# A convolution loop on one core: state products set between two channels, input loaded with batch innermost, gelu written in runs of four

## The chip, the core and the metric

The kernel runs on one core of a Trainium2 chip. The metric is the time on the device in microseconds (us), from launch to the last output, as the median of the runs shown. All inputs lie in HBM; the host only reorders and copies them before the launch, which isn't timed.

## The reference

The input `r` is [8, 2048, 512] (batch, time, channel), float32. Two residual blocks follow each other:

```
x = r
x = x + LN(gelu(causal_conv(LN(x), K) + D * LN(x)))     # block 1
x = x + LN(tanh(LN(x) Wo^T + c_final Uo^T + bo))          # block 2
```

In block 1 every channel has its own kernel K of 2048 taps, given by a state space of 64 complex states; the reference computes it with FFTs. In block 2 `c_final` is the end state of a gated recurrence that runs over the first axis (here the 8 batch entries) with sigmoid and tanh gates, for all 2048 positions at once:

```
c = f * c + i * g,   f, i = sigmoid(x W^T + c U^T + b),   g = tanh(x W^T + c U^T + b)
```

LN subtracts the mean and divides by the standard deviation over the 512 channels, with no learned scale.

## The kernel before, in words

**Set-up and statistics** (`stats`, line 409 on). The powers of the state matrix, the first taps of K and other constants are made by short chains of small instructions. Beside them `stats(j)` takes the time axis in 16 chunks of 128 positions (positions on partitions): two loads bring a chunk's 8 rows per position from `xr` into `xs` (line 421), VectorE's `bn_stats` (L424) and ScalarE's accumulating copies (L429, L433) give mean and 1 / std of each row, which stay in `mu1` and `rs1`. For the first two groups of channels `u`, the normalized input, is made here from `xc` (L442 on GpSimd, L443 on VectorE), split in a float16 high part (L446, ScalarE) and the float16 rest (L447, GpSimd). A scheduler orders the instructions of this stage on each engine.

**The convolution loop** takes 32 channels at a time: 16 groups `g`. A chunk's output is a Toeplitz product of the chunk with the first 128 taps (tile `t`, a load from `kpad`, L494) plus a product of the state before the chunk (tile `x`) with the powers that read the state out (tile `m`). All matrix products are done with both sides split in hi and lo, so three matmuls each (`mm3`, lines 388 to 390: hi hi, lo hi, hi lo). Within a group the work goes by 16 slots, and inside the loop the order on TensorE, ScalarE, VectorE and GpSimd is the order in which the program is written. A slot `s_` of group `g` has:

- `chain_step(g + 1, s_)`: the state after chunk s_ of the next group. Three products of the transition matrix `at` with the state before are added in PSUM (`pxt`); `split` then writes x's high half (L83, ScalarE) and its low half (L84, VectorE). Its third product reads the low half of the previous state.
- `conv_out` in even slots: gelu of the four channels finished in the two slots before (L531, ScalarE), from PSUM `pyt` [position, channel, chunk and batch] into `y` [position, chunk and batch, channel]. The pattern walks PSUM in storage order, so it writes one float32 every 64 bytes. After 16 channels `y` is stored to `y_d`.
- `conv_mm(g, s_)`: two channels, 12 products.
- `tap_step` in slots 1 to 12: the next group's tile `m`, doubled from 4 to 128 columns by three products of 64 to 512 columns, evicted by L83 and L84.
- `chain_in(g + 1, s_ + 1)`: three products of the input matrix `bm` with `u`, the first part of the next `pxt`.
- `norm_x(g + 2, ...)`: the input of the group after next, loaded in `xg` (L453), in four parts: mean off (L466, GpSimd), times 1 / std (L468, VectorE), high part `u` (L470, ScalarE), low part (L472, GpSimd; VectorE for group 2). Two parts fall in a slot, so that in a steady group the even slots have GpSimd's first part and ScalarE's `u`, the odd ones VectorE's and GpSimd's second.

`xr` has, for a chunk, position and group, the 8 batch entries outside and the 32 channels inside; `u` has channels outside and batch inside. So L470 and L472 read `xg` with a step of 128 bytes.

Group 0 has no chain and no taps beside it, group 14 has no `norm_x` but splits weights of the recurrence, group 15 (`conv_last`) goes in two parts of the sequence. All loads and stores of the loop go through SyncE's queue, in an order that the scheduler plans and where a transfer waits for its buffer, and everything behind it in the queue waits too.

**The recurrence** then runs over 8 blocks of 256 positions and 8 steps each (`prep`, `norm`, `turn`, `scan`, `head`). It reads `y_d` and isn't touched by the change.

Of the kernel before, what the change touches and what calls it, by code (L numbers as in the profile page):

```python
# [45 lines left out]
def s4_gated_block(ctx, tc, a, dbg=None):  # L46
# [28 lines left out]
    # long-lived results of the set-up  # L75
# [21 lines left out]
    with ExitStack() as sctx:  # L97
# [10 lines left out]
        # large temporaries sit where later tiles of the convolution will  # L108
# [277 lines left out]
    def mm3(out, w, x, start=True, stop=True):  # L386
        """out (+)= w^T x with both sides as hi + lo: hi hi + hi lo + lo hi"""
        T.matmul(out, lhsT=w(0), rhs=x(0), start=start, stop=False)  # L388
        T.matmul(out, lhsT=w(1), rhs=x(0), start=False, stop=False)  # L389
        T.matmul(out, lhsT=w(0), rhs=x(1), start=False, stop=stop)  # L390

# [12 lines left out]
    with ExitStack() as cctx:  # L404
# [4 lines left out]
        def stats(j):  # L409
            """mean and 1 / std of the rows of chunk j (VectorE and ScalarE share the batch),  # L410
            and u of the first two groups"""
# [6 lines left out]
            for i in range(2):  # L418
                tag = ("y", "xg", "y", "xg", "u2")[(2 * j + i) % 5]
                xh.append((cr if tag == "xg" else ce if tag == "u2" else cb).tile([P, NG, HB, G], F32, name="xs", tag=tag, bufs=1 if tag == "u2" else 2))  # L420
                dma(out=xh[i], in_=a["xr"][j, :, :, i * HB : (i + 1) * HB])
            row = lambda b: xh[b // HB][:, :, b % HB, :]
# [4 lines left out]
            for b in range(na):  # L427
                jk = xp.tile([P, NG, G], F16, name="jk", bufs=1)
                S.activation(jk, row(nd + b), AF.Copy, accum_out=sm[:, 0, b : b + 1])  # L429
            S.mul(sm[:, 1, 0:na], sm[:, 0, 0:na], -1.0 / H)  # L430
            for b in range(na):
                jk = xp.tile([P, NG, G], F16, name="jk", bufs=1)
# [16 lines left out]
        def load_x(g):  # L449
            us[g] = (cb, cr, ce)[g % 3].tile([P, NJ, 2, G, NB], F16, name="u", tag=f"u{g % 3}", bufs=1)  # L450
            for jq in range(NJ // JQ):
                xg = cr.tile([P, JQ, NB, G], F32, name="xg")
                dma(out=xg, in_=a["xr"][jq * JQ : (jq + 1) * JQ, :, g].rearrange("j p b h -> p j b h"))  # L453
                xgs[g, jq] = xg

        def norm_x(g, jp, part):
            """u = LN(x) as [time, chunk, channel, batch], split in hi and lo, in four parts"""
# [5 lines left out]
            x3, xv = xg.rearrange("p j b h -> p (j b) h"), xg.rearrange("p j b h -> p j h b")  # L463
            bc = lambda m: m[:, js, :].rearrange("p j b -> p (j b)")[:, :, None].to_broadcast([P, JP * NB, G])
            if part == 0:
                Q.tensor_tensor(x3, x3, bc(mu1), ALU.subtract)  # L466
            elif part == 1:
                V.tensor_tensor(x3, x3, bc(rs1), ALU.mult)  # L468
            elif part == 2:
                S.activation(u[:, js, 0], xv, AF.Copy)  # L470
            else:
                (V if g == 2 else Q).tensor_tensor(u[:, js, 1], xv, u[:, js, 0], ALU.subtract)  # L472

        def chain_in(g, j):
            """B u of chunk j, the first part of the state after it"""
# [6 lines left out]
        def chain_step(g, j):  # L482
            x, pxt = xs_[g], pxs.pop((g, j))
            if j:
                mm3(pxt, lambda i: at16[:, i, :], lambda i: x[:, j - 1, i, :], start=False)
            split(x[:, j, 0, :], x[:, j, 1, :], pxt)

        def load_taps(g):
            """first-chunk Toeplitz blocks, and the start of the powers that read the state out"""
# [23 lines left out]
        def conv_mm(g, c):  # L513
            """two channels of group g"""
            u, x = us[g], xs_[g]
            if c % 2 == 0:
                pys[g] = py.tile([P, 4, NJ * NB], F32, name="pyt")
            for hg in (2 * c, 2 * c + 1):
                sl, hm = 2 * g + hg // HS, hg % HS
                t0, m = t0s[sl], ms[sl]  # L520
                o = pys[g][:, hg % 4, :]
                mm3(o, lambda i: t0[:, i, :, hm], lambda i: u[:, :, i, hg, :], stop=False)
                mm3(o[:, NB:], lambda i: m[:, i, :, hm], lambda i: x[:, :, i, hg * NB : (hg + 1) * NB], start=False)

        def conv_out(g, c4):
            """gelu of four channels"""
# [4 lines left out]
            S.activation(y[:, :, h4 : h4 + 4].rearrange("p c h -> p h c"), pys[g], AF.Gelu, scale=unsc)  # L531
# [4 lines left out]
        def conv_last(g):  # L536
            """the last group in two parts of the sequence: the first positions can go on earlier"""
            u, x = us[g], xs_[g]
            yt = {}
            for j0, j1, hn in ((0, JF, HS), (JF, NJ, 4)):  # L540
                n = j1 - j0
                for sl in (2 * g, 2 * g + 1):
# [4 lines left out]
                    for h0 in range(0, HS, hn):  # L547
# [7 lines left out]
                        S.activation(y[:, :, h0 : h0 + hn].rearrange("p c h -> p h c"), pyt, AF.Gelu, scale=unsc)  # L555
# [25 lines left out]
        # when the weights' halves are split and loaded: {group: {slot: (splits, loads)}}  # L581
# [10 lines left out]
        for g in range(NG):  # L592
# [16 lines left out]
            with tc.manual_schedule(engines=MAN):  # L609
# [13 lines left out]
                for s_ in range(NJ):  # L623
# [12 lines left out]
                    if nn:  # L636
                        # the loads of group 3 come late: its parts are taken in fewer slots
                        d = ND1 if g == 1 else 0
                        while norms and s_ >= d and (s_ == NJ - 1 or len(norms) > 4 + 2 * NJ * (NJ - 1 - s_) // (NJ - d)):
                            norm_x(g + 2, *norms.pop(0))  # L640
# [15 lines left out]
    def lnstat(src, tag):  # L656
        """mean and 1 / std of the rows of each [P, ...] view in src"""
# [16 lines left out]
    def prep(q, t, cjs=(0, 1)):  # L674
        """x1"""
# [16 lines left out]
    def norm(q, t, cjs=(0, 1)):  # L692
        """its normed rows"""
# [5 lines left out]
    def turn(q, t, cjs=(0, 1)):  # L699
        """the normed rows with channels on partitions, split in hi and lo"""  # L700
# [11 lines left out]
    def scan(q, t, mr=range(KT)):  # L712
        """a step of the recurrence for a block of positions"""
# [33 lines left out]
    def zbank(q):  # L747
        """a PSUM bank of products with positions on partitions (after the scan its banks are free)"""
# [111 lines left out]
def _arrays(d):  # L860
    """The inputs, laid out as the kernel reads them (copies and reorderings only)."""
# [16 lines left out]
    a["xr"] = r[:, :, ::-1].transpose(1, 2, 3, 0, 4)  # L878
# [20 lines left out]
```

## Time and profile before

| | |
|---|---|
| runs before | 2988.52 us median of 3 (2986.27 to 2988.61) |
| span of the profiled execution, first to last instruction | 2986.2 us, 59439 instructions |
| its stages, from the first starts of their lines | set-up and statistics to about 158 us, loop to 643 us, recurrence to the end |
| busy over the span | PE 95%, DVE 56%, ACT 38%, POOL 24% |
| mean granted TensorE clock | 0.982 of full |
| DMA | 311.32 MB, mean 104 GB/s |

The profile shows one execution. The times of the three runs are listed without naming the one that was profiled; its span lies 2.3 us under their median. PE is TensorE's matmuls and PEld its weight loads, DVE is VectorE, ACT ScalarE, POOL GpSimd, SP SyncE. A group of instructions is listed by line, engine, output and input tile with shapes, then count, busy time, mean of one, and the idle time of the engine just before them with what ended it. Matmuls overlap, so their spacing is read from their starts and not from their durations. A row of a table by stretches has the stretch and its length, then busy us and count for PE, PEld, DVE, ACT and POOL, and the granted clock, the share of time in which the DMA engines were busy, and what they moved in GB/s.

### The profile page before, as it was taken

The page shows a single profiled execution, that of the slowest core. Times are in us where ns is not written, and L with a number is a line of the kernel's source. Part 1 is how long each engine was busy: PE and PEld are TensorE (multiplying, and loading weights), DVE is VectorE, ACT ScalarE, POOL GpSimd, SP SyncE. Part 2 cuts the span into 40 slices and gives each one's busy share as a digit, 9 for nine tenths or more (in the row PEclk, how much of TensorE's full clock was granted, in tenths as well). Part 3 has the DMA queues.
Part 4 walks back from the last instruction along what each step waited for, and adds up shares of the span by engine and source line. Part 5 has one row for each costly group of instructions (what it writes and reads, how often), then busy time and mean ns, then how long its engine had stood idle before and what let it go on. Part 6 is the DMA issues. An engine that isn't in the chain of part 4 may idle for free.

```text
span 2986.2 us, 59439 instructions
## 1 busy us (share of the span) xinstructions
PE 2844.7 (95%) x25044; PEld 2346.3 (79%) x25044; DVE 1670.0 (56%) x3674; ACT 1130.7 (38%) x2288; POOL 730.1 (24%) x723
## 2 busy tenths in 40 slices
PE   3589999899999999999999999999999999999998
PEld 2367777788888888788888888887888788888884
DVE  7766666656645555655555555555555655563336
ACT  8888888842222222222222222222222222222221
POOL 5757777600100111111111111111111111110013
PEclk9699999989999999999999999999999999999999
DMA  8977676765522222322232222222222322221003
GB/s 223 280 216 213 204 214 202 203 174 127 107 50 58 71 72 71 78 71 72 71 93 71 72 72 72 71 72 71 72 71 72 85 72 71 71 79 43 29 29 103
DMA packets 520916, 311.32 MB, mean 104 GB/s; under 512 B 282310, under 2 KB 442568, under 8 KB 520648
## 3 DMA queue, kind: packets, MB, share of 16 engines
q1 hardware_dynamic: 520216, 306.99, 38.8%
q8 instruction: 196, 3.21, 0.5%
q14 instruction: 72, 0.59, 0.1%
q10 hardware_dynamic: 432, 0.52, 0.1%
HBM read 206.28 MB, written 101.19 MB: 103 GB/s over the span
## 4 chain that ended last, share of the span: by engine, by line
PE 71%; issue 10%; ACT 6%; DVE 5%; DMA 3%; POOL 2%; POOLq 0%; SPq 0%; ACTq 0%; DVEq 0%
PE pfi L390 12%; PE pfi L388 12%; PE pfi L389 12%; PE pgg L388 6%; PE pgg L389 6%; PE pgg L390 6%; PE pz L389 3%; PE pz L390 3%; PE pz L388 3%; ACT u L470 2%; ACT y L531 2%; PE pt L708 2%; PE pxt L390 1%; DVE xg L468 1%; PE pyt L389 1%
## 5 line engine op out<-in xcount | busy, mean ns | idle before, releaser
L389 PEld LDWEIGHTS <-w 128*128 128x128 f16 x5808 | 568.0, 98 | 73.4 <-issue 6.4
L388 PEld LDWEIGHTS <-w 128*128 128x128 f16 x5808 | 568.0, 98 | 72.3 <-issue 0.7
L390 PEld LDWEIGHTS <-w 128*128 128x128 f16 x5808 | 568.0, 98 | 72.1
L388 PE MATMUL pfi<-xt,w 128*128 128x256 f16 x2048 | 559.8, 273 | 0.7 <-ACT xt L83 0.7
L389 PE MATMUL pfi<-xt,w 128*128 128x256 f16 x2048 | 559.9, 273 | 0.0
L390 PE MATMUL pfi<-xt,w 128*128 128x256 f16 x2048 | 559.6, 273 | 0.1
L388 PE MATMUL pfi<-ch,w 128*128 128x256 f16 x1792 | 489.1, 273 | 5.1 <-ACT ch L742 5.1
L390 PE MATMUL pfi<-ch,w 128*128 128x256 f16 x1792 | 489.0, 273 | 0.1
L389 PE MATMUL pfi<-ch,w 128*128 128x256 f16 x1792 | 489.1, 273 | 0.0
L731 ACT ACTIVATE gate<-pfi,bias 128x256 f32<-128x256 f32 x512 | 214.8, 471 | 644.0 <-PE pfi L390 643.3
L737 DVE SCALAR_TENSOR_TENSOR a<-gate,cd 128x256 f32<-128x256 f32 x224 | 118.1, 527 | 508.5 <-ACT gate L731 508.5
L667 POOL TENSOR_TENSOR rsh<-rsh,nhalf 128x2 f32<-128x2 f32 (+1 forms) x65 | 45.1, 693 | 1458.6 <-DVE rsh L666 1436.4
L742 ACT ACTIVATE ch<-cd 128x256 f16<-128x256 f32 x256 | 106.6, 416 | 530.6 <-DVE cd L741 530.6
L388 PE MATMUL pgg<-xt,w 128*128 128x256 f16 x1024 | 279.1, 273 | 0.0
L389 PE MATMUL pgg<-xt,w 128*128 128x256 f16 x1024 | 279.1, 273 | 0.0
L390 PE MATMUL pgg<-xt,w 128*128 128x256 f16 x1024 | 279.1, 273 | 0.0
L389 PE MATMUL pgg<-ch,w 128*128 128x256 f16 x896 | 244.3, 273 | 0.0
L388 PE MATMUL pgg<-ch,w 128*128 128x256 f16 x896 | 244.3, 273 | 0.0
L390 PE MATMUL pgg<-ch,w 128*128 128x256 f16 x896 | 244.2, 273 | 0.0
L83 ACT ACTIVATE xt<-pt 128x512 f16<-128x512 f32 x128 | 75.8, 597 | 316.6 <-PE pz L390 218.6
L779 POOL TENSOR_TENSOR x1r<-x1r,h 128x512 f32<-128x512 f32 x124 | 181.2, 1480 | 41.1 <-DVE h L778 41.1
L740 DVE SCALAR_TENSOR_TENSOR gate<-gate,gate 128x256 f32<-128x256 f32 x256 | 108.9, 426 | 137.4 <-ACT gate L731 137.4
(303 smaller groups left out, 5964.2 us busy)
## 6 DMA issues: line engine op xcount, KB each, us to landing
xs<-in_xr SPq DMA_DIRECT2D x32, 1024.0 KB, 8.5
t<-kpad SPq DMA_DIRECT2D x32, 1024.0 KB, 5.3
xr<-in_r SPq DMA_DIRECT2D x128, 256.0 KB, 3.4
x_d<-x SPq DMA_DIRECT2D x128, 256.0 KB, 3.5
x1r<-x_d SPq DMA_DIRECT2D x128, 256.0 KB, 3.4
out<-x1r SPq DMA_DIRECT2D x128, 256.0 KB, 2.0
y<-y_d SPq DMA_DIRECT2D x62, 512.0 KB, 5.6
y_d<-y SPq DMA_DIRECT2D x30, 1024.0 KB, 6.4
```

The lines of the kernel that those rows point to most:

```text
L83: S.activation(hi, src, AF.Copy)
L388: T.matmul(out, lhsT=w(0), rhs=x(0), start=start, stop=False)
L389: T.matmul(out, lhsT=w(1), rhs=x(0), start=False, stop=False)
L390: T.matmul(out, lhsT=w(0), rhs=x(1), start=False, stop=stop)
L470: S.activation(u[:, js, 0], xv, AF.Copy)
L531: S.activation(y[:, :, h4 : h4 + 4].rearrange("p c h -> p h c"), pys[g], AF.Gelu, scale=unsc)
L708: T.transpose(pt[:, k], xn[:, k * P : (k + 1) * P], ident)
L731: S.activation(r, outs[gt], AF.Tanh, scale=gsc[gt], bias=bs[:, gt, m : m + 1])
L737: V.scalar_tensor_tensor(a2, gate[0], 1.0, cst_[q, t - 1, m], ALU.add, ALU.mult)
L740: V.scalar_tensor_tensor(gate[1], gate[1], 1.0, gate[2], ALU.add, ALU.mult)
L742: S.activation(ch[:, 0], cd, AF.Copy, scale=0.5)
L779: (V if (q, t) >= (NQB - 1, NB - 2) else Q).tensor_tensor(x1r, x1r, hv[cj], ALU.add)
```

## The change

Five edits, all ahead of the recurrence:

1. `xr` has batch innermost; `norm_x` works on [chunk, channel, batch], with mean and 1 / std running along the batch.
2. The statistics load whole rows from a second copy of the input, `rr`, in which a position's rows of 512 channels follow each other; `xc` is laid out [channel, batch], written by GpSimd with a step.
3. The gelu (also in `conv_last`) walks its output in storage order, in runs of four channels, and reads PSUM with a step of 512 bytes.
4. `chain_step` is cut in `chain_hi`, the two products with the high half of the state before, and `chain_lo`, the product with its low half and the split. `conv_mm` does one channel. A slot sets `chain_hi` between its two channels and `chain_lo` after the second.
5. The parts of `norm_x` stand ahead of the slot's channels, not at its end.

```diff
-                xh.append((...).tile([P, NG, HB, G], F32, name="xs", ...))
-                dma(out=xh[i], in_=a["xr"][j, :, :, i * HB : (i + 1) * HB])
-            row = lambda b: xh[b // HB][:, :, b % HB, :]
+                xh.append((...).tile([P, HB, H], F32, name="xs", ...))
+                dma(out=xh[i], in_=a["rr"][j, :, i * HB : (i + 1) * HB])
+            row = lambda b: xh[b // HB][:, b % HB, :]
...
-            xc = xp.tile([P, 2, NB, G], F32, name="xc")
+            xc = xp.tile([P, 2 * G, NB], F32, name="xc")
...
-                Q.tensor_tensor(xc[:, :, bs], xh[i][:, 0:2], mu1[:, None, j, bs, None].to_broadcast([P, 2, HB, G]), ALU.subtract)
-            V.tensor_tensor(xc, xc, rs1[:, None, j, :, None].to_broadcast([P, 2, NB, G]), ALU.mult)
+                Q.tensor_tensor(xc[:, :, bs].rearrange("p h b -> p b h"), xh[i][:, :, 0 : 2 * G], mu1[:, j, bs, None].to_broadcast([P, HB, 2 * G]), ALU.subtract)
+            V.tensor_tensor(xc, xc, rs1[:, j, None, :].to_broadcast([P, 2 * G, NB]), ALU.mult)
             for g in range(2):
-                xv = xc[:, g].rearrange("p b h -> p h b")
+                xv = xc[:, g * G : (g + 1) * G]
...
-                xg = cr.tile([P, JQ, NB, G], F32, name="xg")
+                xg = cr.tile([P, JQ, G, NB], F32, name="xg")
...
-            bc = lambda m: m[:, js, :].rearrange("p j b -> p (j b)")[:, :, None].to_broadcast([P, JP * NB, G])
+            bc = lambda m: m[:, js, None, :].to_broadcast([P, JP, G, NB])
             if part == 0:
-                Q.tensor_tensor(x3, x3, bc(mu1), ALU.subtract)
+                Q.tensor_tensor(xg, xg, bc(mu1), ALU.subtract)
             elif part == 1:
-                V.tensor_tensor(x3, x3, bc(rs1), ALU.mult)
+                V.tensor_tensor(xg, xg, bc(rs1), ALU.mult)
             elif part == 2:
-                S.activation(u[:, js, 0], xv, AF.Copy)
+                S.activation(u[:, js, 0], xg, AF.Copy)
             else:
-                (V if g == 2 else Q).tensor_tensor(u[:, js, 1], xv, u[:, js, 0], ALU.subtract)
+                (V if g == 2 else Q).tensor_tensor(u[:, js, 1], xg, u[:, js, 0], ALU.subtract)
...
-        def chain_step(g, j):
+        def chain_hi(g, j):
+            if j:
+                for i in range(2):
+                    T.matmul(pxs[g, j], lhsT=at16[:, i, :], rhs=xs_[g][:, j - 1, 0, :], start=False, stop=False)
+
+        def chain_lo(g, j):
             x, pxt = xs_[g], pxs.pop((g, j))
             if j:
-                mm3(pxt, lambda i: at16[:, i, :], lambda i: x[:, j - 1, i, :], start=False)
+                T.matmul(pxt, lhsT=at16[:, 0, :], rhs=x[:, j - 1, 1, :], start=False, stop=True)
             split(x[:, j, 0, :], x[:, j, 1, :], pxt)
...
-            S.activation(y[:, :, h4 : h4 + 4].rearrange("p c h -> p h c"), pys[g], AF.Gelu, scale=unsc)
+            S.activation(y[:, :, h4 : h4 + 4], pys[g].rearrange("p h c -> p c h"), AF.Gelu, scale=unsc)
...
-                    if ahead and s_ < NJ - 1:
-                        chain_step(g + 1, s_)
                     if s_ % 2 == 0 and s_:
                         conv_out(g, s_ // 2 - 1)
-                    conv_mm(g, s_)
+                    if nn:
+                        d = ND1 if g == 1 else 0
+                        while norms and s_ >= d and (...):
+                            norm_x(g + 2, *norms.pop(0))
+                    conv_mm(g, 2 * s_)
+                    if ahead and s_ < NJ - 1:
+                        chain_hi(g + 1, s_)
+                    conv_mm(g, 2 * s_ + 1)
+                    if ahead and s_ < NJ - 1:
+                        chain_lo(g + 1, s_)
                     if ahead and 1 <= s_ <= 12:
                         tap_step(*taps[s_ - 1])
                     if ahead and s_ < NJ - 2:
                         chain_in(g + 1, s_ + 1)
-                    if nn:
-                        ...
...
-    a["xr"] = r[:, :, ::-1].transpose(1, 2, 3, 0, 4)
+    a["xr"] = r[:, :, ::-1].transpose(1, 2, 3, 4, 0)
+    a["rr"] = g("L0_attn_r").reshape(NB, NJ, P, H)[:, :, ::-1].transpose(1, 2, 0, 3)
```

In the set-up stage the scheduler also places some instructions anew; on SyncE's queue the first three loads of `t` come ahead of the two halves of the last chunk of `xs`, where they came behind them.

More of the change, by code (lines that the diff above doesn't have):

```diff
@@ L419, in stats @@
                 tag = ("y", "xg", "y", "xg", "u2")[(2 * j + i) % 5]
-                xh.append((cr if tag == "xg" else ce if tag == "u2" else cb).tile([P, NG, HB, G], F32, name="xs", tag=tag, bufs=1 if tag == "u2" else 2))
-                dma(out=xh[i], in_=a["xr"][j, :, :, i * HB : (i + 1) * HB])
-            row = lambda b: xh[b // HB][:, :, b % HB, :]
+                xh.append((cr if tag == "xg" else ce if tag == "u2" else cb).tile([P, HB, H], F32, name="xs", tag=tag, bufs=1 if tag == "u2" else 2))
+                dma(out=xh[i], in_=a["rr"][j, :, i * HB : (i + 1) * HB])
+            row = lambda b: xh[b // HB][:, b % HB, :]
             for b in range(nd):
@@ L427, in stats @@
             for b in range(na):
-                jk = xp.tile([P, NG, G], F16, name="jk", bufs=1)
+                jk = xp.tile([P, H], F16, name="jk", bufs=1)
                 S.activation(jk, row(nd + b), AF.Copy, accum_out=sm[:, 0, b : b + 1])
@@ L431, in stats @@
             for b in range(na):
-                jk = xp.tile([P, NG, G], F16, name="jk", bufs=1)
+                jk = xp.tile([P, H], F16, name="jk", bufs=1)
                 S.activation(jk, row(nd + b), AF.Square, bias=sm[:, 1, b : b + 1], accum_out=sm[:, 2, b : b + 1])
@@ L451, in load_x @@
             for jq in range(NJ // JQ):
-                xg = cr.tile([P, JQ, NB, G], F32, name="xg")
-                dma(out=xg, in_=a["xr"][jq * JQ : (jq + 1) * JQ, :, g].rearrange("j p b h -> p j b h"))
+                xg = cr.tile([P, JQ, G, NB], F32, name="xg")
+                dma(out=xg, in_=a["xr"][jq * JQ : (jq + 1) * JQ, :, g].rearrange("j p h b -> p j h b"))
                 xgs[g, jq] = xg
@@ L462, in norm_x @@
             u, xg = us[g], xgs[g, j0 // JQ][:, j0 % JQ : j0 % JQ + JP]
-            x3, xv = xg.rearrange("p j b h -> p (j b) h"), xg.rearrange("p j b h -> p j h b")
-            bc = lambda m: m[:, js, :].rearrange("p j b -> p (j b)")[:, :, None].to_broadcast([P, JP * NB, G])
+            bc = lambda m: m[:, js, None, :].to_broadcast([P, JP, G, NB])
             if part == 0:
-                Q.tensor_tensor(x3, x3, bc(mu1), ALU.subtract)
+                Q.tensor_tensor(xg, xg, bc(mu1), ALU.subtract)
             elif part == 1:
-                V.tensor_tensor(x3, x3, bc(rs1), ALU.mult)
+                V.tensor_tensor(xg, xg, bc(rs1), ALU.mult)
             elif part == 2:
-                S.activation(u[:, js, 0], xv, AF.Copy)
+                S.activation(u[:, js, 0], xg, AF.Copy)
             else:
-                (V if g == 2 else Q).tensor_tensor(u[:, js, 1], xv, u[:, js, 0], ALU.subtract)
+                (V if g == 2 else Q).tensor_tensor(u[:, js, 1], xg, u[:, js, 0], ALU.subtract)
         def chain_in(g, j):
@@ L480, in chain_in, with chain_step @@
             mm3(pxs[g, j], lambda i: bm16[:, i, :], lambda i: u[:, j, i, :], stop=(j == 0))
-        def chain_step(g, j):
+        def chain_hi(g, j):
[3 more added lines that the diff above has]
+        def chain_lo(g, j):
             x, pxt = xs_[g], pxs.pop((g, j))
             if j:
-                mm3(pxt, lambda i: at16[:, i, :], lambda i: x[:, j - 1, i, :], start=False)
+                T.matmul(pxt, lhsT=at16[:, 0, :], rhs=x[:, j - 1, 1, :], start=False, stop=True)
             split(x[:, j, 0, :], x[:, j, 1, :], pxt)
+        def chain_step(g, j):
+            chain_hi(g, j)
+            chain_lo(g, j)
         def load_taps(g):
@@ L511, in tap_steps, with conv_mm @@
             return [(sl, lv, k) for lv, k in steps for sl in (2 * g, 2 * g + 1)]
-        def conv_mm(g, c):
+        def conv_mm(g, hg):
             u, x = us[g], xs_[g]
-            if c % 2 == 0:
+            if hg % 4 == 0:
                 pys[g] = py.tile([P, 4, NJ * NB], F32, name="pyt")
[L518 to L523, printed above, removed]
+            sl, hm = 2 * g + hg // HS, hg % HS
+            t0, m = t0s[sl], ms[sl]
+            o = pys[g][:, hg % 4, :]
+            mm3(o, lambda i: t0[:, i, :, hm], lambda i: u[:, :, i, hg, :], stop=False)
+            mm3(o[:, NB:], lambda i: m[:, i, :, hm], lambda i: x[:, :, i, hg * NB : (hg + 1) * NB], start=False)
         def conv_out(g, c4):
@@ L554, in conv_last @@
                                 lambda i: x[:, max(j0 - 1, 0) : j1 - 1, i, hg * NB : (hg + 1) * NB], start=False)
-                        S.activation(y[:, :, h0 : h0 + hn].rearrange("p c h -> p h c"), pyt, AF.Gelu, scale=unsc)
+                        S.activation(y[:, :, h0 : h0 + hn], pyt.rearrange("p h c -> p c h"), AF.Gelu, scale=unsc)
                     d = dma(out=y_d[j0:j1, :, sl].rearrange("j p b h -> p j (b h)"), in_=y.rearrange("p (j b) h -> p j (b h)", b=NB))
@@ L626, in s4_gated_block @@
                             yload(0, cj, 0, slice(0, 2 * g))
-                    if ahead and s_ < NJ - 1:
-                        chain_step(g + 1, s_)
                     if s_ % 2 == 0 and s_:
                         conv_out(g, s_ // 2 - 1)
-                    conv_mm(g, s_)
+                    if nn:
+                        d = ND1 if g == 1 else 0
+                        while norms and s_ >= d and (s_ == NJ - 1 or len(norms) > 4 + 2 * NJ * (NJ - 1 - s_) // (NJ - d)):
+                            norm_x(g + 2, *norms.pop(0))
[5 more added lines that the diff above has]
+                        chain_lo(g + 1, s_)
                     if ahead and 1 <= s_ <= 12:
@@ L635, in s4_gated_block @@
                         chain_in(g + 1, s_ + 1)
-                    if nn:
-                        d = ND1 if g == 1 else 0
-                        while norms and s_ >= d and (s_ == NJ - 1 or len(norms) > 4 + 2 * NJ * (NJ - 1 - s_) // (NJ - d)):
-                            norm_x(g + 2, *norms.pop(0))
                     if g in wjobs:
```

## The prediction

> **What bounds the kernel now.** I read the 40 slices of the page, then cut the span by stages, then took the costliest shapes, the waits and the timeline of the stage that the change touches. Three stages stand out: set-up with statistics up to about 158 us, the convolution loop over 16 channel groups to 643 us, and the recurrence to 2986 us. The recurrence (2343 us, TensorE busy in nearly every slice) has none of the changed lines, so only the first 643 us can move.
>
> Busy time by stretch (us, then PE, PEld, DVE, ACT, POOL; granted clock, DMA share, GB/s): two stretches of the set-up, group 0, and two of the steady groups:
> ```profile
> 75.00:100.00 25.00, 14.72 (x54) 8.96 (x55) 21.66 (x69) 24.52 (x72) 20.61 (x34) 0.57 1.18 291
> ...
> 158.00:188.20 30.20, 25.35 (x312) 23.30 (x310) 19.27 (x30) 23.59 (x33) 12.41 (x13) 0.89 0.66 202
> ...
> 308.80:338.90 30.10, 28.13 (x317) 23.32 (x316) 19.89 (x35) 25.98 (x45) 22.75 (x19) 1.00 0.71 211
> 338.90:369.00 30.10, 28.13 (x317) 23.31 (x316) 19.95 (x35) 26.01 (x45) 22.78 (x19) 1.00 0.72 210
> ```
> The steady groups repeat to 0.2%. DMA is far from full there, so PE, ACT or the handing over between them sets the 30.15 us.
>
> Shapes of the loop, from 230 to 560 us (count | busy us, mean ns | idle before):
> ```profile
> L472 POOL TENSOR_TENSOR u<-xg,u 128x512 f16<-128x512 f32 x88 | 133.3, 1521 | 83.2 <-ACT u L470 83.2
> L470 ACT ACTIVATE u<-xg 128x512 f16<-128x512 f32 x88 | 102.3, 1162 | 0.6
> L468 DVE TENSOR_TENSOR xg<-xg,rs 128x512 f32<-128x512 f32 x88 | 101.3, 1151 | 6.7 <-POOL xg L466 6.7
> L531 ACT ACTIVATE y<-pyt,unsc 128x512 f32<-128x512 f32 x88 | 100.5, 1143 | 0.0
> ...
> L83 ACT ACTIVATE m<-pmt 128x512 f16<-128x512 f32 x66 | 39.4, 598 | 11.4 <-PE pmt L390 10.2
> ```
> Three ACT rows have the same 512 elements. The one that reads and writes in storage order takes 598 ns; the two that step (u reads every 128 bytes, the gelu writes every 64 bytes) take 1162 and 1143.
>
> Two slots of a steady group, ACT and then DVE and PE:
> ```profile
> 412.45 1.16 ACT L470 ACTIVATE u<-xg 128x512 f16<-128x512 f32 x1
> 413.50 0.39 ACT L83 ACTIVATE x<-pxt 128x256 f16<-128x256 f32 x1
> 414.02 0.60 ACT L83 ACTIVATE m<-pmt 128x512 f16<-128x512 f32 x1
> 414.70 0.39 ACT L83 ACTIVATE x<-pxt 128x256 f16<-128x256 f32 x1
> 414.98 1.13 ACT L531 ACTIVATE y<-pyt,unsc 128x512 f32<-128x512 f32 x1
> 416.10 0.60 ACT L83 ACTIVATE m<-pmt 128x512 f16<-128x512 f32 x1
> 416.74 1.15 ACT L470 ACTIVATE u<-xg 128x512 f16<-128x512 f32 x1
> ```
> ```profile
> 415.26 1.45 DVE L468 TENSOR_TENSOR xg<-xg,rs 128x512 f32<-128x512 f32 x1
> 416.63 0.41 DVE L84 TENSOR_TENSOR x<-pxt,x 128x256 f16<-128x256 f32 x1
> ...
> 417.09 0.27 PE L390 MATMUL pxt<-x,at 128*128 128x256 f16 x1 [0.49 <-DVE x L84]
> ```
> Every second slot carries gelu and u on ACT, 2.3 us, beside the x and m copies; the next slot's state product waits for the x copy queued behind them, or for DVE's half of x behind the 1.45 us xg product.
>
> The PE floor of a group, from starts in the PE timeline at full clock: one channel of conv_mm 0.365 us, three 256-column products 0.33, a tap of 64, 128, 256 or 512 columns 0.08, 0.17, 0.33, 0.65. That is 32 x 0.365 + 15 x 0.33 (chain_in) + 14 x 0.33 (chain_step) + 2 x 0.08 + 2 x 0.17 + 2 x 0.33 + 6 x 0.65 = 26.3 us. So 3.85 us of each of 13 groups (1 to 13; (580 - 188) / 30.15 = 13) are stalls: 50 us is all that the loop can give.
>
> **The change part by part.** *The copy u.* With batch innermost in xr, u reads in storage order. The nearest row is m at 598; I take 0.60, so -0.56 x 8 = -4.5 us of ACT per group. POOL's L472 has the same step; it should fall toward L466's 1.28 (mean, same size), -0.24 x 8 = -1.9 us of POOL, which DVE's xg product also feels, since its 1.15 is a mean between 0.74 and 1.47. The mean and scale operands of L466 and L468 now run along the batch instead of standing still; I cost that at nothing, bound +-0.2 us each: POOL is idle 7 us of 30 and DVE 10, but a longer L468 would sit straight in front of DVE's x.
>
> *The gelu.* It now writes 16-byte runs, but reads PSUM every 512 bytes. No row here reads PSUM with a step. By storage order it would be m's 0.60 plus what a per-partition operand adds (L433's 719 against L429's 627: 0.09), 0.69. By the nearest stepped row (SBUF, u) it stays at 1.16. [...]by storage order -3.65. I take 0.69: [...] It is a narrow choice, and 1.16 is the second case below. Ends kept: 0.65 and 2.2.
>
> *The order in a slot.* Before: state products (3), gelu, two channels, tap, chain_in, then the normalizing parts. After: gelu and the normalizing parts, channel one, the two products with x's high half, channel two, the one with its low half, tap, chain_in. No instruction is added; each product is the same 0.11 us. From the end of the last state product to the next product with the high half there are now a tap, chain_in and one channel, 0.65 + 0.33 + 0.365 = 1.35 us in tap slots (1.71 before) and 0.70 in slots without. What is needed is PE's 0.27, ACT's 0.39 and handing over, about 0.70: met, with nothing to spare without a tap. For the low half the distance is 0.22 + 0.365 more, 1.93 and 1.28 against about 1.22 needed. The gain is on the other side: from the tap to x's copy PE now has chain_in, two channels and three products, 1.4 us instead of 0.66, in which ACT does m, gelu and u (0.60 + 0.69 + 0.60 less overlap, 1.7) and DVE its m half and xg (0.69 + 1.15). So ACT delivers x about 0.2 us late in a 512-column slot, where 0.65 is spare. In slots without tap, m is absent and ACT is on time. What is late next is DVE's x half behind xg: 0.1 to 0.3 us in the odd slots where POOL slows xg. I leave 1.1 us of the 3.85 in a group (eight slot pairs at 0.1, and 0.3 at the seam between groups). Loop: -2.75 x 13 = -36 us. If the cover of that 0.65 us goes, each gelu/u pair costs what it exceeds it by.
>
> *Group 0.* No chain runs beside it; from 163 to 181 us the chain of waits is gelu and u in turn on ACT, 16 copies. They shrink to 8 x 1.29 = 10.3, under the 32 x 0.365 = 11.7 us of PE; with the fill that is about 14 us for 18: -4.
>
> *Statistics.* ACT loses 2 x 0.25 us a chunk (633 to x<-pxt's 384), 8 us of some 137 busy; POOL gives up as much in the stepped write of xc as it gets back in u. The load of a half chunk goes from 512-byte to 8-KB runs. [...] By the trace, 512-byte loads make 291 GB/s at a share of 1.18, and the 1- and 4-KB mix between 140 and 160 us makes 317 at 0.94; over the 43 us in which this queue is full that is 43 x (1 - 291/317) = 3.5 us. ACT is as full there (24.52 of 25), so I count 1.5. Against it: in SP's queue the three first tap loads now stand ahead of the last chunk's two halves. They wait for the kernel's own write to kpad (11.4 us to landing) and bring 3 MB, about 10 us at 300 GB/s, onto the engines before xs; what waits is the last bn_stats, with DVE's x halves queued behind it. The chain of states ends only at 162.9 us anyway, 4 to 5 us after that chunk's u, so some 5 us show, less the ACT gain. Set-up together: +1.5, from -10 to +8.
>
> *Group 14 and 15.* Weight loads fill the DMA queue (share 1.01) in 14, nothing normalizes; -0.5. The last group's gelus wait for PE; only the last counts, -0.5.
>
> Sum: -36 - 4 + 1.5 - 1 = -39.5. The profiled span is 2986.2 us, 2.3 under the median of 2988.52; 2946.7 against the span is 2949 against the median.
>
> **The rivals.** *Gelu stays at 1.16.* [...] An ACT pair is then 0.47 longer; in 512-column slots x arrives with 0.05 us left, in short slots 0.2 to 0.3 late. I leave 1.95 a group instead of 1.1: -1.9 x 13 = -25, group 0 -3, the rest +1: -27, 2961 us.
>
> *DVE and set-up take it back.* The wait for x's low half was the larger PE wait already (12.6 us against 7.1 for the high half), and its distance in short slots is unchanged. The loop gives 1.3 x 13 = 17, group 0 gives 4, and set-up costs 8 to 10: about -12, 2976 us. Against it: POOL's contiguous copy shortens the overlap.
>
> *Slower: the stepped PSUM read costs more than the stepped write did.* Place: ACT, even slots, ahead of x. At 2.2 us, u saves 4.5 a group and gelu adds 8 x 1.05 = 8.4; ACT needs 26.0 + 3.9 = 29.9 and keeps half of its 4.1 us of waits for PE: 32, +1.8 x 13 = +23, group 0 +4, set-up +1.5: 3016 us. It decides from a gelu of about 1.14 + 0.56 = 1.70 us. Against it: no ACT row with a step costs more than twice the dense one.
>
> **How the numbers follow.** Likeliest 0.50 (2949), gelu unchanged 0.27 (2961), taken back 0.14 (2976), slower 0.09 (3016). The range runs from the likeliest with 10 us from set-up and a floor-bound loop, 2930, to just past the third, 2978. Within 0.2%, 6 us, about what a measurement of this kernel can tell from no change: 0.05, from the ends of the third case and the fourth. Faster: 0.86; slower 0.09.
>
> **What would show it.** Right: u on ACT near 0.6 and gelu near 0.7; steady groups of 27 to 28 us; ACT idle before x, waiting for PE; PE waits under 1.2 us a group and nearly all for DVE's x; group 0 under 15 us; the conv start within 8 us of 158. Wrong: gelu over 1.1 us; groups over 29 us with ACT still full; L468 longer than 1.2 us with the low-half product behind it; a first convolution product after 166 us; or anything in the recurrence longer than its 2343 us.

## The result, and the profile after

| | before | after |
|---|---|---|
| median of four runs | 2988.07 us (2986.27 to 2988.61) | 2950.55 us (2949.5 to 2954.2) |
| ratio, 95% interval | | 0.9877 [0.9865, 0.9889] |
| profiled execution, its span | 2986.2 us | 2952.4 us (the run of 2954.2) |
| steady group, from the starts of the `y_d` stores of groups 5 to 12 | 30.16 us | 27.94 us |
| last `y_d` store of the loop | 644.03 us | 611.01 us |

The change brings 37.5 us, and 2949 was predicted. The profiled execution of after is the slowest of its four, 3.65 us over their median, so the traces account for 33.8 us. Almost all of it is there when the loop ends: the last store comes 33.0 us earlier. What follows it, 2342 us of recurrence, gives the other 0.8.

The profile after, by stretches (busy us of PE, PEld, DVE, ACT and POOL, granted clock, DMA share, GB/s): the same stretch of the set-up as before, and two steady groups.
```profile
75.00:100.00 25.00, 12.13 (x42) 5.83 (x40) 21.63 (x66) 22.90 (x70) 19.86 (x37) 0.50 0.88 314
...
293.70:321.65 27.95, 26.78 (x317) 23.70 (x316) 20.45 (x37) 19.08 (x43) 21.60 (x19) 1.00 0.75 227
321.65:349.60 27.95, 26.78 (x318) 23.71 (x316) 20.48 (x37) 19.08 (x43) 21.94 (x19) 1.00 0.77 227
```
ACT needs 19.1 us of a group instead of 26.0, and is no longer near the bound. In the set-up the same 25 us move 314 GB/s at a DMA share of 0.88, instead of 291 at 1.18.

The shapes of the loop from 230 to 530 us (count | busy us, mean ns | idle before):
```profile
L465 POOL TENSOR_TENSOR xg<-xg,mu 128x512 f32<-128x512 f32 x87 | 123.6, 1426 | 1.9 <-DMA xg<-in_xr 1.9
L467 DVE TENSOR_TENSOR xg<-xg,rs 128x512 f32<-128x512 f32 x87 | 108.3, 1245 | 12.1 <-POOL xg L465 12.1
L471 POOL TENSOR_TENSOR u<-xg,u 128x512 f16<-128x512 f32 x86 | 104.8, 1223 | 64.7 <-ACT u L469 64.2
...
L540 ACT ACTIVATE y<-pyt,unsc 128x512 f32<-128x512 f32 x86 | 59.2, 688 | 0.0
L469 ACT ACTIVATE u<-xg 128x512 f16<-128x512 f32 x86 | 54.2, 630 | 22.4 <-DVE xg L467 22.4
```
The gelu went from 1143 to 688 ns, u from 1162 to 630, GpSimd's low part from 1521 to 1223. The two normalizing instructions ahead of them went the other way: VectorE's product from 1151 to 1245, and GpSimd's mean subtraction from 1277 to 1426. The row of the subtraction before, from 230 to 560 us:
```profile
L466 POOL TENSOR_TENSOR xg<-xg,mu 128x512 f32<-128x512 f32 x88 | 112.0, 1277 | 0.0
```
What TensorE waits for between 230 and 510 us (total us, times, longest), before and then after:
```profile
PE pxt L390 <- DVE x L84: 8.4, 19, 0.5
PE pxt L388 <- ACT x L83: 5.3, 18, 0.4
```
```profile
PE pxt L491 <- DVE x L84: 11.2, 10, 1.1
```
After, it is one wait of 1.1 us a group, always at the same place. The two totals, 13.7 and 11.2 us, lie closer together than the groups do, because this view counts idle time alone: a product of 256 columns is shown 0.27 us long although the next one can start 0.11 us after it, so a short wait does not appear. Read from the starts of the matmuls, with the spacing of experiment 6 as the measure, the state products of a steady group start 3.6 us late in all before and 1.4 us after. Without that, both groups would take 26.6 us.

The timeline of the wait, from the second slot of a group into the third, shows its chain; the bracket gives the idle time and its releaser:
```profile
324.89 0.75 POOL L507 COPY m<-mb 128x128 f16<-128x128 f16 x1
...
325.61 2.54 POOL L465 TENSOR_TENSOR xg<-xg,mu 128x512 f32<-128x512 f32 x2
...
326.64 0.38 ACT L83 ACTIVATE x<-pxt 128x256 f16<-128x256 f32 x1
...
326.93 1.78 DVE L467 TENSOR_TENSOR xg<-xg,rs 128x512 f32<-128x512 f32 x1 [1.09 <-POOL xg L465]
...
328.62 0.41 DVE L84 TENSOR_TENSOR x<-pxt,x 128x256 f16<-128x256 f32 x1
...
329.09 0.27 PE L491 MATMUL pxt<-x,at 128*128 128x256 f16 x1 [1.11 <-DVE x L84]
```
ACT's half of x is there at 327.0. VectorE's half could follow at once, but the product of `norm_x` stands ahead of it in VectorE's order. That product waits 1.09 us for GpSimd's subtraction (and GpSimd had a copy of `m` to do first), runs 1.78 us beside GpSimd, and the low half of x starts 1.6 us late.

The start of the convolution, on PE and POOL:
```profile
153.83 0.22 PE L388 MATMUL pyt<-u,t 128*128 128x128 f16 x1 [3.08 <-ACT u L446]
...
159.45 0.27 PE L390 MATMUL pyt<-u,t 128*128 128x128 f16 x1 [5.34 <-POOL u L447]
```
```profile
153.85 4.92 POOL L465 TENSOR_TENSOR xg<-xg,mu 128x512 f32<-128x512 f32 x4 [1.25 <-DMA xg<-in_xr]
158.73 1.31 POOL L447 TENSOR_TENSOR u<-xc,u 128x256 f16<-128x256 f32 x2
```
The chain of states ends at 150.8 us instead of 162.9, but the third product of the first channel waits for the last chunk's low part of u, which GpSimd makes only after four mean subtractions of group 2.

### The profile page after: what moved, and what is told of

The parts are those of the page before. It is cut to its first block, busy times and chain, and to the rows that moved or that the text cites. A ratio compares the mean times of both kernels' runs of the same rounds, so it can differ in the third digit from the quotient of the medians.

```text
span 2952.4 us, 59431 instructions
## 1 busy us (share of the span) xinstructions
PE 2828.6 (96%) x25044; PEld 2353.3 (80%) x25044; DVE 1670.6 (57%) x3674; ACT 1017.7 (34%) x2288; POOL 718.5 (24%) x723
## 4 chain that ended last, share of the span: by engine, by line
PE 74%; issue 10%; DVE 4%; DMA 3%; POOL 3%; ACT 1%; POOLq 0%; SPq 0%; DVEq 0%; ACTq 0%
PE pfi L390 12%; PE pfi L389 12%; PE pfi L388 12%; PE pgg L389 6%; PE pgg L388 6%; PE pgg L390 6%; PE pz L390 3%; PE pz L389 3%; PE pz L388 3%; PE pt L721 2%; PE pyt L389 2%; PE pyt L390 2%; PE pyt L388 1%; DVE xg L467 1%; DMA wl<-in_wt 1%
```

## The experiments

All ratios are to the kernel before, run beside each, with 95% intervals. "Group" is the steady group of each profile, read as in the table above. What follows the last `y_d` store is the same work in every kernel and takes from 2340 to 2344 us in these profiles, so a difference of a few us in one span is not yet a difference of the loop.

**The changed kernel again.** 

> The changed kernel itself, on the same chip as the three others, so that differences of a few us between variants can be read. Both theories: 2950 to 2952 us, steady group 27.95 us.

2950.82 us, 0.9875 [0.9861, 0.9890].

**1. The gelu alone undone**

```diff
-S.activation(y[:, :, h4 : h4 + 4], pys[g].rearrange("p h c -> p c h"), AF.Gelu, scale=unsc)
+S.activation(y[:, :, h4 : h4 + 4].rearrange("p c h -> p h c"), pys[g], AF.Gelu, scale=unsc)
```
(and the same in `conv_last`)

> The changed kernel with the gelu alone put back: it walks PSUM in storage order and writes one float32 every 64 bytes. Theory (the two ACT copies carry the gain, the loop now lies near PE's floor with spare time on ACT): gelu goes from 688 back to about 1147 ns; the ACT pair of gelu and u grows by 0.46 us and uses most of the spare time, so a steady group goes from 27.95 to about 28.8 us (my second case said 0.85 more a group), group 0 loses 2 us: about 2962 us. Rival (the order of the slot carries the gain, ACT was never the bound): ACT has 9 us idle in a group of 28, 3.7 more fit in, group within 0.2 us of 27.95: 2951 to 2953 us.

2962.98 us, 0.9916 [0.9901, 0.9931]; gelu 1151 ns, group 28.79 us. The pattern of the gelu is worth 12 us, 0.85 us a group, which is a quarter of the 8 x 0.46 us that it takes off ACT.

**2. The layout of `xr` and `norm_x` alone undone**

```diff
-xg = cr.tile([P, JQ, G, NB], F32, name="xg")
+xg = cr.tile([P, JQ, NB, G], F32, name="xg")
...
-a["xr"] = r[:, :, ::-1].transpose(1, 2, 3, 4, 0)
+a["xr"] = r[:, :, ::-1].transpose(1, 2, 3, 0, 4)
```


> The changed kernel with the input of norm_x alone put back to channels innermost (u and its low half read with a step of 128 bytes, mean and 1 / std stand still along the inner axis); the statistics keep whole rows. Theory (ACT copies): u back to 1162 ns, 0.53 us more in each even slot in front of x, group about 28.9 us, 2963 us. Rival A (slot order): group within 0.2 us, 2951 to 2953 us. Rival B (GpSimd's mean subtraction got slower by the change, 1037 to 1260 ns at least, and sits at the seam between groups ahead of VectorE's product and x): it gets faster again, the seam's 1.1 us wait shrinks, group 27.3 to 27.9 us, 2942 to 2950 us.

2958.15 us, 0.9900 [0.9885, 0.9915]; u 1138 ns, group 28.44 us. It is worth 7.5 us, where 12 were expected: the long u comes back, but at the wait of the changed kernel the two mean subtractions take 1.05 us each again, where they took 1.28 and 1.29. TensorE's waits for VectorE's x fall from 11.2 to 2.6 us in 280, and 6.4 us of waits for ScalarE's x come in their place. (Over the whole run the subtraction is not shorter: its median is 1501 ns, against 1290 in the changed kernel.)

**3. The statistics alone undone** (loads by channel group from a copy in the old order, and `xc` with batch outside, as before)

```diff
-dma(out=xh[i], in_=a["rr"][j, :, i * HB : (i + 1) * HB])
+dma(out=xh[i], in_=a["xo"][j, :, :, i * HB : (i + 1) * HB])
...
```


> The changed kernel with the statistics alone put back: half chunks loaded in 512-byte runs from a copy of the input in the old layout, xc with batch outside, u of the first two groups read with a step. The loop is as changed. Theory (set-up gains a little: 0.5 us of ACT a chunk and faster loads, less what the new queue order costs): the first full convolution product comes 3 to 8 us later than in the changed kernel, 2953 to 2959 us. Rival (the set-up is bound by its own chains and nothing of edit 2 shows): within 2 us of the changed kernel.

2956.90 us, 0.9891 [0.9876, 0.9906], against 0.9875 [0.9861, 0.9890] of the changed kernel beside it. The first store of `y_d` comes at 172.24 us (168.34 after, 172.00 before), the group is 27.94 in both. The loads are again what they were before: 282 GB/s at a DMA share of 1.14 from 75 to 100 us, and 8.7 us to landing. The traces show 3.9 us at the start of the loop, 1.5 us of it at the end of group 13, and none at the last store, which comes at 610.28 us here and at 611.01 in the changed kernel; the two intervals overlap. That whole rows are loaded faster and start the loop earlier is shown; how much of it stays, between nothing and 6 us, is not settled.

**4. The order of a slot alone undone** (edits 4 and 5: `chain_step` at the head, the parts of `norm_x` at the end)

```diff
+                    if ahead and s_ < NJ - 1:
+                        chain_step(g + 1, s_)
...
-                    if nn:
-                        ...norm_x(g + 2, *norms.pop(0))
-                    conv_mm(g, 2 * s_)
-                    if ahead and s_ < NJ - 1:
-                        chain_hi(g + 1, s_)
-                    conv_mm(g, 2 * s_ + 1)
-                    if ahead and s_ < NJ - 1:
-                        chain_lo(g + 1, s_)
+                    conv_mm(g, 2 * s_)
+                    conv_mm(g, 2 * s_ + 1)
...
+                    if nn:
+                        ...norm_x(g + 2, *norms.pop(0))
```


> The changed kernel with the slot order alone put back: three state products first, then gelu, two channels, tap, chain_in, normalizing parts. All layouts stay as changed. Theory (ACT copies carry it): of the 3.85 us lost per group before, 0.5 to 0.8 us per even slot came from gelu and u in front of x; with 1.0 us less of them most of it goes without the new order: group about 28.2 us, 2954 us. Rival (order carries it): group about 29.6 us, 2972 us.

2957.03 us, 0.9898 [0.9883, 0.9913], group 28.10. With the new layouts the two edits of the order together bring 6 us.

**5. The order of a slot alone done**, on the kernel before (edits 4 and 5, the diff of experiment 4 the other way, with the old layouts, gelu and statistics)

> The kernel before with the slot order alone changed (state products split between the two channels, normalizing parts ahead); layouts, gelu and statistics stay as before. Theory (ACT copies): gelu and u still take 2.3 us in an even slot, now both between m and x; group 29.6 to 30.3 us, 2980 to 2990 us. Rival (order carries it): group about 28.5 us, 2967 us.

2995.76 us, 1.0028 [1.0019, 1.0037]: slower than before, and slower than was expected. The group is 31.05 us. TensorE's waits from 230 to 510 us:
```profile
PE pxt L486 <- ACT x L83: 24.8, 51, 1.0
PE pyt L390 <- DVE x L84: 1.6, 9, 0.2
```
and ACT's timeline of one even slot:
```profile
413.95 1.13 ACT L541 ACTIVATE y<-pyt,unsc 128x512 f32<-128x512 f32 x1
414.87 1.11 ACT L470 ACTIVATE u<-xg 128x512 f16<-128x512 f32 x1
415.86 0.40 ACT L83 ACTIVATE x<-pxt 128x256 f16<-128x256 f32 x1
```
Gelu and u both stand between two copies of x; the products for this copy had started at 414.16 and 414.76, so x waits for its turn on ACT. The order needs either a shorter pair of copies or a pair that does not stand together in front of x. The next three runs tell which.

**6. The changed kernel with the parts of `norm_x` behind `chain_lo`**, ahead of the tap

```diff
-                    if nn:
-                        ...norm_x(g + 2, *norms.pop(0))
                     conv_mm(g, 2 * s_)
...
                         chain_lo(g + 1, s_)
+                    if nn:
+                        ...norm_x(g + 2, *norms.pop(0))
                     if ahead and 1 <= s_ <= 12:
```


> The changed kernel with the normalizing parts moved from ahead of the slot's channels to behind chain_lo (ahead of the tap). Theory (what is left in the loop is VectorE's product xg, 1.77 us while GpSimd works, in front of x's low half once per group at the seam): x's half goes first, the 1.1 us wait at the seam is gone, group 27.95 to about 27.0 us, about 2939 us. Rival (the wait moves: xg now stands in front of the tap's half m, or GpSimd's mean subtraction itself is late): group within 0.3 us of 27.95, 2947 to 2955 us.

2933.92 us, 0.9814 [0.9799, 0.9828]: 17 us faster than the changed kernel, from one block moved by a few lines. Two groups (columns as above):
```profile
286.20:312.80 26.60, 26.54 (x316) 23.63 (x316) 19.38 (x36) 19.16 (x45) 21.97 (x19) 1.00 0.79 239
312.80:339.40 26.60, 26.54 (x316) 23.63 (x316) 19.26 (x36) 19.13 (x44) 21.74 (x19) 1.00 0.79 238
```
ACT and POOL are as busy as in the changed kernel, to 0.4 us; PE is busy all but 0.06 us of the 26.60, and between 230 and 510 us the trace has no wait of PE for another engine. The wait of the changed kernel at the seam between two groups is gone, as this stretch of VectorE at the same place of a group shows:
```profile
341.81 0.42 DVE L84 TENSOR_TENSOR x<-pxt,x 128x256 f16<-128x256 f32 x1 [1.55 <-ACT x L83]
342.15 0.99 DVE L467 TENSOR_TENSOR xg<-xg,rs 128x512 f32<-128x512 f32 x1
343.07 0.21 DVE L84 TENSOR_TENSOR m<-pmt,m 128x64 f16<-128x64 f32 x1
343.29 0.42 DVE L84 TENSOR_TENSOR x<-pxt,x 128x256 f16<-128x256 f32 x1
```
The product now comes after x's low half, and has a slot to finish before the next.

**7. The same place, with the old layouts**: the kernel of experiment 5 with the same block moved behind `chain_lo`

> The kernel before with the slot order of the change (chain_hi between the two channels, chain_lo after the second), its own layouts of input and gelu, and the parts of norm_x at the end of the slot behind chain_lo. The same order with these parts at the slot's head took 2995.8 us. If the place of the parts in front of x is what made the order cost 7 us, u (1.16 us) no longer stands between a slot's gelu and its x on ScalarE, the waits for ACT x fall from 25 us in 290 to under 10, groups are 29.0 to 29.8 us and the time 2974 to 2984 us. If ScalarE's load is what decides (26 us of copies against a TensorE floor of 26.3), the waits only move to the next slot, and it stays at 30.5 us or more and 2990 to 2997 us.

2951.49 us, 0.9881 [0.9867, 0.9896], group 27.42: far better than either theory had it. This kernel has none of the changed layouts, its ACT copies are the long ones of before, and it is as fast as the changed kernel (0.9875 [0.9861, 0.9890]). Two groups, then ACT over two slots:
```profile
293.00:320.40 27.40, 26.94 (x317) 23.68 (x316) 18.18 (x36) 25.48 (x44) 24.13 (x19) 1.00 0.76 232
320.40:347.80 27.40, 26.93 (x317) 23.68 (x315) 18.15 (x36) 25.49 (x44) 24.12 (x19) 1.00 0.77 228
```
```profile
412.40 1.18 ACT L470 ACTIVATE u<-xg 128x512 f16<-128x512 f32 x1 [0.21 <-DVE xg L468]
413.47 0.22 ACT L83 ACTIVATE m<-pmt 128x64 f16<-128x64 f32 x1
413.58 0.39 ACT L83 ACTIVATE x<-pxt 128x256 f16<-128x256 f32 x1
413.84 0.29 ACT L83 ACTIVATE m<-pmt 128x128 f16<-128x128 f32 x1
414.00 1.21 ACT L541 ACTIVATE y<-pyt,unsc 128x512 f32<-128x512 f32 x1
414.96 0.46 ACT L83 ACTIVATE x<-pxt 128x256 f16<-128x256 f32 x1
```
There is a copy of x between u and gelu: the pair is taken apart. ACT is busy 25.5 of 27.4 us, and TensorE waits for its x only 4.1 us in 280. So ACT's load was not the bound by itself; the place of the long copies in front of x was.

**8. The fifth edit alone undone**: the parts at the very end of the slot, behind tap and `chain_in`, where they were before

> The changed kernel with its fifth edit alone undone: the parts of norm_x stand again at the end of the slot, behind the tap and chain_in, where the kernel before had them. If it is enough that they do not stand between a slot's gelu and its x, groups are 26.5 to 26.8 us and the time 2932 to 2938 us, as with the parts directly behind chain_lo (2933.9). If they have to come before the tap, since here u and xg run on into the next slot's x, a part of the 1.4 us of a group comes back: groups of 27.2 to 27.9 us, 2942 to 2951 us.

2938.42 us, 0.9832 [0.9815, 0.9848], group 26.65. The fifth edit by itself, as the change made it, costs 12 us. The fourth by itself, with the new layouts, brings 19 us (2957.0 in experiment 4, 2938.4 here); the 6 us of experiment 4 are the difference of the two. The end of the slot is 4.5 us slower in the median than the place behind `chain_lo`, with intervals that overlap.

Experiments 4 to 7 with the kernels before and after make a table (median us, and group us). "Layouts" are edits 1 to 3.

| | old slot order | new order, `norm_x` at the head | new order, `norm_x` behind `chain_lo` |
|---|---|---|---|
| old layouts | 2988.1 (30.16) | 2995.8 (31.05) | 2951.5 (27.42) |
| new layouts | 2957.0 (28.10) | 2950.6 (27.94) | 2933.9 (26.59) |

**9. Mean and 1 / std operands standing still**, in the changed kernel

```diff
-bc = lambda m: m[:, js, None, :].to_broadcast([P, JP, G, NB])
+bc = lambda m: m[:, js, 0:1, None].to_broadcast([P, JP, G, NB])
```


> The changed kernel with the mean and 1 / std operands of norm_x standing still: the value of batch entry 0 is taken for all eight, so that part of the normalization is left out for groups 2 to 15; instructions, sizes and order are those of the changed kernel. If the operand that runs along the batch is what lengthened them, GpSimd's mean subtraction (L465) falls from a least 1.26 and mean 1.43 us to the 1.04 and 1.28 of before, VectorE's L467 from 1.24 to 1.15, groups from 27.95 to about 27.6 and the time to 2945 to 2948 us. If it is contention of the two engines at their new places that lengthens both, the durations stay within 0.05 us and the time within 2 us of 2950.7.

2942.74 us (2939.09 to 2948.10), 0.9853 [0.9838, 0.9868], group 27.19. The row of the mean subtraction over the whole run (least / median / longest ns), in this run and then in the changed kernel:
```profile
L465 POOL TENSOR_TENSOR xg<-xg,mu x112: 1032/1045/1510, 141.9 to 530.2; 128x512 f32<-128x512 f32 x112
```
```profile
L465 POOL TENSOR_TENSOR xg<-xg,mu x112: 1260/1290/1750, 144.1 to 544.7; 128x512 f32<-128x512 f32 x112
```
The instruction has the same size, engine and layout of its large operand. Only the small operand differs: standing still, or running over 8 values again and again. That is 0.22 us of each of GpSimd's subtractions. VectorE's product shows nothing of it in its least time (681 and 682 ns); its mean in the loop falls from 1245 to 1108, with GpSimd's shorter work beside it. TensorE's wait at the seam falls from 11.2 to 4.6 us in 280, and the group by 0.75 us. The median is 8 us under that of the changed kernel; the four runs lie 9 us apart and the intervals overlap, so the size in the whole time is less certain than in the group.

**10. The last chunk's low part of u on VectorE**, in the changed kernel

```diff
-Q.tensor_tensor(us[g][:, j, 1], xv, us[g][:, j, 0], ALU.subtract)
+(V if j == NJ - 1 else Q).tensor_tensor(us[g][:, j, 1], xv, us[g][:, j, 0], ALU.subtract)
```


> The changed kernel with the low half of u of the last chunk of the statistics made by VectorE and not by GpSimd. Theory (in the changed kernel the first convolution product with that half waits 5.3 us, because GpSimd has four mean subtractions of group 2 queued in front of it): the wait shrinks to under 1 us, the loop starts 4 us earlier, 2946 us. Rival (group 0 then waits for something else, such as the loads of group 3, or the start doesn't carry through): within 2 us of the changed kernel.

2949.18 us, 0.9863 [0.9846, 0.9879]. The wait of 5.34 us is gone, and the first and the last store of `y_d` both come 6.3 us earlier than in the profile after. The span is only 3.9 us shorter and the median 1.6 less than that of the changed kernel beside it, with intervals that overlap. The cause of the late start is shown; that removing it shortens the run is not, on its own.

**11. Experiments 6 and 10 together**

> The changed kernel with both edits that helped: the parts of norm_x behind chain_lo, and the low part of u of the last chunk on VectorE. If the two places are independent (one in the loop, one ahead of it), the gain of the second, 1.6 us on its own, adds to the 2933.9 us of the first: 2931 to 2933, groups 26.55 us, first y_d store near 162 us. If what the second brings is swallowed by the loads of group 3 and 4 that POOL waits for early in the loop, 2934 us with a first store at 162 us all the same. Slower than 2936 us would speak against either.

2927.07 us (2926.05 to 2934.05), 0.9798 [0.9781, 0.9814]: the fastest of these kernels, 2% under before. Against experiment 6 alone it is 7 us less in the median, more than expected, but their intervals overlap, and the traces do not show it: the first store of `y_d` comes 2.4 us earlier (163.6 against 166.0, where 162 was expected) and the last 0.9 us later. What is certain is the gain of experiment 6.

## Why the prediction was right, and where not

**The durations.** The gelu was taken at 0.69 us and took 0.688; u at 0.60 and took 0.630; the low part on GpSimd was to fall toward 1.28 and fell to 1.22. The narrow choice was the gelu's read of PSUM every 512 bytes. No row of before has such a read, and that it costs no more than a dense one was the author's estimate. The measured 688 ns are what was worked out for a dense read (m's 597 ns and the 0.09 us by which L433 is longer than L429; a gelu that is dense on both sides was not run). The slower rival, which needed a gelu over 1.70 us, fell with that row. The rival "gelu stays at 1.16" had its own experiment: 2961 worked out, 2963 measured. The end agrees better than its parts: the group was put at 28.2 us and is 28.8, and the set-up gave back what that missed.

**The loop, -36 us in the sum, was too much.** From the end of group 0 to that of group 13 the stores move from 5.76 to 33.37 us earlier: 27.6 us in 13 groups, 2.1 each instead of 2.75. The steady group is 27.94 where 27.4 was worked out. Three terms are off. The TensorE floor was put at 26.3; experiment 6, in which TensorE hardly waits, runs at 26.6. The residual stall was put at 1.1 us, as 0.1 in each of eight slot pairs and 0.3 at the seam. It is next to nothing in the pairs and 1.35 at the seam: L491 would have started 0.06 us behind the matmul before it, at 327.82, and started at 329.09, and one more product of a group is 0.08 late. And group 1, which the sum took as a steady one, gains nothing: 38.0 us before, 39.4 after.

**A step that failed is the operand costed at nothing.** The sum named the mean operand of L466, gave it a bound of 0.2 us either way, and took nothing because GpSimd is idle 7 us of 30. It costs 0.22 us a subtraction, and experiment 9, in which the operand of VectorE's product stands still too, shows 0.75 us of a group. The idle share was no cover: at the seam two subtractions stand one after the other, VectorE waits for the first, and x waits for VectorE. The sentence that a longer L468 "would sit straight in front of DVE's x" was right, and should have entered the sum for L466 too. It is also the one of the listed signs of being wrong that came: L467 takes 1.245 us in the mean, over the 1.2 that were named, and the low-half product stands behind it.

**The order in a slot was worked as one step, and is two.** The prediction counted what ACT has between the tap and x (m, gelu and u, 1.7 us), found x 0.2 late with 0.65 to spare, and left it. That held: in the changed kernel TensorE does not wait for ACT. Put with the old copies, 0.60 + 1.15 + 1.16 = 2.9 us, or 2.7 with the same overlap, the count leaves x about 0.65 us later than the cover allows, and experiment 5 shows such waits: 0.5 us in the mean, 1.0 at most. What was not seen is that in the new order it is the fifth edit that puts u into this queue: the order of the state products with the parts behind `chain_lo` brings 36 us with no layout changed (experiment 7), and with the parts at the head it is 44 us slower than that. By the table the layouts bring 31 us in the old order, where they shorten what stands in front of x, 45 us with the parts at the head, and 17.6 with the parts behind, where the group then runs at TensorE's floor.

**Set-up and group 0: -2.5 in the sum, -5.8 in the trace** (the second store). The gain of the loads was halved from 3.5 to 1.5 and the queue order charged 5. The trace has the loads at 314 GB/s (317 was the estimate from the mixed stretch), 7.1 us to landing instead of 8.5; experiment 3, with the old runs, has the old figures. GpSimd was taken to lose as much in the stepped write of `xc` as it gets back in u: the write went from 612 to 658 ns in the median, u's low part from 806 to 668, two of each a chunk. The charge for the three tap loads was wrong: SP issues them at 120.6 us and the last chunk at 122.4, when before that chunk was issued only after 129.6, so they delayed nothing that showed. The chain of states then ends 12 us earlier; 5.3 us are lost again to the four subtractions ahead of the last u on GpSimd (experiment 10). This queue, which the prediction passed over, is the new wait of the set-up.

**Groups 14 and 15 and the last gelu** were put at -1 and gave +0.4. **The third case**, set-up and VectorE taking it back (2976), had the right engine: the wait that is left is VectorE's half of x. Its size was not: the loop kept 2.1 us a group instead of 1.3, and the set-up gained where it was to cost 8.

**The sum as a whole.** The medians, 2949 predicted and 2950.55 measured, agree better than the working does. Between the profiled spans the sum said -39.5 and the traces have -33.8: the gain of the loop was put 8 us too high and that of the set-up and group 0 3 us too low, and the profiled execution of after ran 3.65 us over its median. The durations and the direction were right, and so was the wait that is left. That the total came so near is in part luck: the two edits of the order, which the prediction costed as one, bring 19 us and take 12 back.

## What to carry to other kernels

Where engines run in program order, ask of each instruction that is moved what it now stands in front of. A block that nobody needs soon cost 1.4 us of a group (short copies) to 3.6 us (long copies) when it stood in front of the value that the next step of the loop needs, as against the place behind it. That is as much as the new layouts brought. Before an engine that is 86% busy is called the bound, look whether others wait for all of its work, or only for one instruction that stands behind long ones. When a layout is turned so that the large operand runs well, cost the small broadcast operand too (here 0.22 us of each subtraction), at the one place where its engine is late, not by its idle share.

## What the runs showed of the hardware

- GpSimd's subtraction of 128x512 float32 took at least 1032 ns (experiment 9) and 1037 (before) with a mean operand that stands still along the inner axis, and 1260 (after) with one that runs over 8 values; VectorE's product shows no such difference in its least time (681 in experiment 9, 682 after).
- ScalarE's gelu of 128x512 float32 took 688 ns (after) with PSUM read every 512 bytes and SBUF written in 16-byte runs, and 1151 with PSUM read in order and one value written every 64 bytes (experiment 1). Its copy of the same size took 630 ns (after) from SBUF in order and 1138 with a read every 128 bytes (experiment 2).
- VectorE's float32 product of the same shape took from 682 to 1777 ns in the run of after: 683 to 685 in the five that hardly overlap a GpSimd instruction, 712 to 1777 in the 62 that lie wholly beside GpSimd's work. In the timeline of after, the low half of x behind such a product of 1.78 us starts at 328.62 us, 1.6 us after ScalarE's half of it is there.
- Loads of 1 MB in 8-KB runs took 7.1 us to landing in the median, where 512-byte runs took 8.5 (8.7 in experiment 3); from 75 to 100 us the former moved 314 GB/s at a DMA share of 0.88, the latter 291 at 1.18 (282 at 1.14).
